# A density stage's tail: ScalarE writes the x term of two of three layer-1 sums into PSUM, with another order of the queues

## The chip, the cores and the metric

The kernel runs on one core of a Trainium2 chip. The metric is the device time of one execution in microseconds. Before the change it is 4800.04 us, the median of three runs (4797.65 to 4801.9). One further execution was profiled; every time by line or engine below is from it, counted from the start of its span.

## What is computed

The input x is 8 images of 192 channels and 64 x 64 pixels, in float32. Two layers follow each other, each with a residual:

```python
x = x + _L0_conv_ref(_gn(x), ...)   # softmax attention over the 4096 pixels
x = x + _L1_conv_ref(_gn(x), ...)   # density: a small network per channel
```

`_gn` is a group norm. The second layer is what the change touches. For every channel it evaluates a network of widths 1, 3, 3, 3, 1 at v - 0.5 and at v + 0.5 (v the normed value), and takes the difference of two sigmoids:

```python
for i in range(N_LAYERS):
    logits = jnp.einsum('cij,cjn->cin', jax.nn.softplus(ms[i]), logits) + bs[i]
    if i < N_LAYERS - 1:
        logits = logits + jnp.tanh(fs[i]) * jnp.tanh(logits)
...
likelihood = jnp.maximum(likelihood, 1e-06)
```

All weights are per channel, that is per partition: every product by a weight is a scale by a [128,1] operand, or, on TensorE, a matmul with a diagonal matrix.

## The kernel before, in words

A channel triple's three channels (g = 0, 1, 2) lie side by side on one of 64 partitions, and the two halves of the image fill 128 partitions. The attention of image b runs in 128 steps (16 steps for each of 8 blocks of 512 rows): scores (L780, PE), Exp (L784, ScalarE), row maxima for a later block (L708 on PE, L716 on VectorE) and the product with the values (L795, PE). The density of image b - 1 is worked off beside the attention of image b. The last image has nothing to run beside, so its density is the tail of the kernel.

The density of an image is 12 units, one for each chunk c of the image (2), g (3) and side s (lower or upper, 2); a unit's tiles are 128 x 1024. In the tail (`on_pe`, the last image) a unit does:

- u_j = tanh(w x + b), j = 0..2: three ScalarE operations (`tanh0`, L1015).
- Three layer-1 sums, one after the other (`product`, L988): sum i is the x term plus three u terms, each a matmul with a diagonal (`diag`, written by ScalarE at L877 and L885), for two halves of 512 columns: 4 x 2 = 8 matmuls, which the trace lists as 16 records. A sum fills two PSUM banks (a `[128, 2, 512]` tile). There are four such tiles in the tail (b0, b1, sc_tail, mx_tail), taken in turn.
- l1_i = tanh(sum i + bias) (`tanh1`, L996, ScalarE, PSUM to SBUF), then l1_i = tanh(f) * l1_i + sum i (`gate1`, L1006, VectorE), which gives the PSUM tile back.
- Three layer-2 sums: the first term with its offset is a ScalarE operation (`scaled`, L1040), the other two are VectorE's (`more`, L1047, in a dependent pair); then tanh (L1030) on ScalarE and the gate (`gate`, L1047 with `tf`).
- The layer-3 sum z: L1040 again and another pair at L1047.

When both sides of a (c, g) have their z, an ending follows. In the tail it is VectorE's and ScalarE's alone (`alone`): z0 + z1 (L1227, here the pair total), tanh of both (L1233), their difference and mask (L1239, L1240), Abs (L1249), and the store step (L1254), after which two DMAs on SP write the result. For the image before, whose last unit reaches into the tail, the last term of z comes from a ScalarE product (`plain`, L1072) that POOL adds in two halves (L1078), each preceded by a small memset (L1163) that waits for a recent VectorE operation.

Each engine runs its queue strictly in the order in which the program was written, so that order decides. It is made by a planner written in Python: `density_step` gives every engine a credit per emission step (`rate`, 4.15 in the tail) and each operation takes its cost (`COST`, in microseconds: DVE 1.22, ACT 1.23, TANH 1.05, PE 6.95). In the order ScalarE, PE, VectorE, up to four units are asked in turn to put operations out (`Unit.step`): the next one of a queue goes if what it needs was put out in an earlier step (VectorE's own results in the same step count as well), if a PSUM tile is free for a sum, and if, where it takes one of the 17 SBUF buffers, more are free than the older units still hold a claim to (`need`). `work_off` first runs what is due, such as endings, then `density_step` and `pool_step`, which puts out at most one waiting POOL piece per step.

```python
if makes and len(bufs) <= sum(u.need() for u in older) + len(endings):
    return
```

Of the kernel before, what the change touches and what calls it, by code (L numbers as in the profile page):

```python
# [10 lines left out]
AF = mybir.ActivationFunctionType  # L11
# [6 lines left out]
def kernel(  # L18
# [43 lines left out]
    nc = tc.nc  # L62

    B, C, H, W = x.shape
# [53 lines left out]
    for i in range(3):  # L118
        t = xin.tile([128, 3, P], F32, tag=f"xi{i}", name=f"xi{i}")
# [58 lines left out]
    for i in range(2):  # L178
        nc.vector.tensor_reduce(
            out=bb[i], in_=ident[:, 64 * i + CR : 64 * i + 64 : 32], axis=AX.X, op=ALU.add  # L180
# [6 lines left out]
    for s in range(2):  # L187
        p = slice(R * s, R * s + R)
# [4 lines left out]
    for i in range(2):  # L193
# [3 lines left out]
        for k in range(2):  # L197
            a = a2 if k == i else a1
            nc.scalar.dma_start(
                out=slope[i][64 * k : 64 * k + 64], in_=a.partition_broadcast(64)  # L200
# [33 lines left out]
    for src, dst, at, n in (  # L234
# [4 lines left out]
        for s in range(2):  # L239
            nc.sync.dma_start(  # L240
                out=dst[R * s : R * s + R, :, at : at + n],
# [91 lines left out]
    credit = {"DVE": 0.0, "ACT": 0.0, "PE": 0.0}  # L333
# [20 lines left out]
    for k in "ab":  # L354
        pair = []
        for i in range(2):
            u = work.tile([128, 2 * C], F32, tag=f"pr{k}{i}", name=f"pr{k}{i}")
# [60 lines left out]
    def work_off(t, rate):  # L418
        now[0] = t
        run_due(t)  # L420
        start_job(t)
        run_due(t)
        held = set()
        for kind, fn in list(loads):
            if free[kind] > 0 and kind not in held:
                loads.remove((kind, fn))
                fn()
            else:
                held.add(kind)
        density_step(t, rate)  # L430
        pool_step()
# [3 lines left out]
    norms = {}  # L435
# [169 lines left out]
    for i in range(2):  # L605
        t = dram.tile([NC, 64, F], F32, tag=f"qd{i}", name=f"qd{i}")
# [259 lines left out]
    COST = {"DVE": 1.22, "ACT": 1.23, "TANH": 1.05, "PE": 6.95}  # L866
    diag = []
    banks = deque()
    lower2 = mm.rearrange("p g n -> p (g n)")[:, 0:36].rearrange("p (s g i) -> p s g i", s=4, g=3)

    def diagonals(g, t):
# [36 lines left out]
    class Unit:  # L908
# [3 lines left out]
        def __init__(self, b, c, g, s):  # L912
            self.key = b, c, g, s
            self.at = {}
            self.buf = {}
            self.todo = {"DVE": deque(), "ACT": deque(), "PE": deque()}
            self.left = {"l": 6, "t": 9, "u": 0, "z": 1, "p": 1}
            self.held = {"l": 0, "t": 0, "u": 0, "z": 0, "p": 0}
            self.on_pe = b == B - 1
            add = self.add  # L920
            if self.on_pe:

                self.left.update(t=3, u=3, p=0)
                for i in range(3):
                    add("ACT", ("u", 0, i), [], self.tanh0, makes="u")
                for i in range(3):
                    add(
                        "PE", ("sum", i), [("u", 0, j) for j in range(3)], self.product,
                        frees=[("u", 0, j) for j in range(3)] if i == 2 else [],
                    )  # L930
                    add("ACT", ("l", 1, i), [("sum", i)], self.tanh1, makes="l")
                for i in range(3):
                    add("DVE", ("gate", 1, i), [("l", 1, i)], self.gate1)
            else:
                for i in range(3):
                    add("ACT", ("t", 0, i), [], self.tanh0, makes="t")
                    add("ACT", ("l", 1, i), [], self.linear, makes="l")
                for i in range(3):
                    for j in range(3):
                        add(  # L940
                            "DVE", ("mix", i, j), [("t", 0, j), ("l", 1, i)], self.mix,
                            frees=[("t", 0, j)] if i == 2 else [],
                        )
                    add("ACT", ("t", 1, i), [("mix", i, 2)], self.tanh, makes="t")
                for i in range(3):
                    add("DVE", ("gate", 1, i), [("t", 1, i)], self.gate, frees=[("t", 1, i)])
            for i in range(3):
                add("ACT", ("l", 2, i), [("gate", 1, 0)], self.scaled, makes="l")
                for j in (1, 2):
                    add("DVE", ("add", 2, i, j), [("gate", 1, j), ("l", 2, i)], self.more)  # L950
                add("ACT", ("t", 2, i), [("add", 2, i, 2)], self.tanh, makes="t")
            for i in range(3):
                add("DVE", ("gate", 2, i), [("t", 2, i)], self.gate, frees=[("t", 2, i)])
            add("ACT", ("l", 3, 0), [("gate", 2, 0)], self.scaled, makes="z")
            add("DVE", ("add", 3, 0, 1), [("gate", 2, 1), ("l", 3, 0)], self.more)
            if self.on_pe:
                add("DVE", ("add", 3, 0, 2), [("gate", 2, 2), ("l", 3, 0)], self.more)
            else:

                add("ACT", ("p", 3, 2), [("gate", 2, 2), ("add", 3, 0, 1)], self.plain, makes="p")  # L960

        def add(self, eng, name, after, fn, makes=None, frees=()):
            self.todo[eng].append((name, after, fn, makes, frees))
# [15 lines left out]
        def src(self):  # L979
            b, c, g, s = self.key  # L980
            return xc[b, c][:, g, :]

        def product(self, k):
            g, i = self.key[2], k[1]
            out = self.buf[k] = banks.popleft()
            for n, src in enumerate([self.src()] + [self.buf["u", 0, j] for j in range(3)]):
                for h in range(2):
                    nc.tensor.matmul(  # L988
                        out[:, h, :], lhsT=diag[g][:, 3 * i + n - 1 if n else 9 + i, :],
                        rhs=src[:, h * F : h * F + F], start=n == 0, stop=n == 3,  # L990
                    )

        def tanh1(self, k):
            b, c, g, s = self.key
# [99 lines left out]
        def need(self):  # L1094
            most = dict(self.left, t=max(0, min(self.left["t"], 1 - self.held["t"])))
            if ("add", 2, 2, 2) not in self.at:

                most.update(z=0, p=0)
            return sum(most.values())

        def step(self, eng, t, older):
            todo = self.todo[eng]
            while todo and credit[eng] > 0:
                name, after, fn, makes, frees = todo[0]
                if any(self.at.get(a, t) >= t for a in after if eng != "DVE" or a[0] in "ltu"):
                    return
                if eng == "PE" and not banks:
                    return
                if makes and len(bufs) <= sum(u.need() for u in older) + len(endings):
                    return  # L1110
                todo.popleft()
                if makes:
                    self.take(name, makes)
                fn(name)
                self.at[name] = t
                for k in frees:
                    self.give(k)
                credit[eng] -= COST["TANH" if name[0] == "t" and name[1] else eng]
# [35 lines left out]
    pieces = deque()  # L1154
# [3 lines left out]
    def pool_step():  # L1158


        if pieces:
            if len(recent) == 2:
                inst = nc.gpsimd.memset(pause, 0.0)  # L1163
                tc.add_manual_dep(
                    inst.ins, recent[0].ins.name,
                    mybir.DependencyInfo(
                        mybir.DependencyClass.Sync, mybir.DependencyReason.DATA
                    ),
                    reason="beside the reduce",
                )  # L1170
            pieces.popleft()()

    def ending(b, c, g):
# [46 lines left out]
        def alone():  # L1220

            s = cell["s"]
            parts = halves if (b, c, g) == (B - 1, 1, 2) else [slice(0, 2 * F)]

            def first():
                for n in parts:
                    nc.vector.tensor_tensor(s[:, n], z[0][:, n], z[1][:, n], ALU.add)  # L1227
                later(1, second, 0.0, 2.1)

            def second():  # L1230
                for n in parts:
                    for i in range(2):
                        nc.scalar.activation(z[i][:, n], z[i][:, n], AF.Tanh, scale=0.5)  # L1233
                later(1, third, 2.5)

            def third():
                for n in parts:
                    y = z[0][:, n]
                    nc.vector.tensor_tensor(y, z[1][:, n], y, ALU.subtract)  # L1239
                    nc.vector.scalar_tensor_tensor(y, s[:, n], 0.0, y, ALU.not_equal, ALU.mult)  # L1240
                bufs.extend((s, z[1]))
                later(1, lambda: size(parts), 0.0, 1.1)
                later(2, lambda: store(parts), 1.3)

            later(1, first, 1.25)
# [151 lines left out]
    RATE = 4.15  # L1397
    scores(0)()
    for t in range(last):
        b = t // IMG  # L1400
# [21 lines left out]
    t = last  # L1422
    homes[:] = [(turns[1], [0, 0])]
    while due or units or jobs or loads:

        work_off(t, RATE if (B - 1, 1) in norms else 1.3)
        t += 1
# [1 line left out]

# [36 lines left out]
```

## Time and profile before

| | us |
|---|---|
| median of three runs | 4800.04 |
| profiled execution | 4801.53 |
| its span | 4799.7 |
| PE busy in the span | 4653.4 (97%) |
| VectorE busy | 4179.0 (87%) |
| ScalarE busy | 3196.8 (67%) |
| POOL busy | 856.3 (18%) |
| first matmul of a layer-1 sum of the tail | at 4470.9 |
| last one | ends at about 4766.5 |
| first L1006 of the tail | at 4492.1 |
| first L1227 of the last image's endings | at 4572.6 |
| last L1227 | at 4788.9 |

Some 1.8 us of the profiled execution lie around its span. A line of the timeline has the start, the duration, the engine, the line of the kernel, the operation with its tiles, and in brackets how long the engine stood idle before it and who ended that. Lines are merged where one line's operations follow each other (x2, x3). Consecutive operations of an engine overlap by about 0.1 us, so the step from one start to the next is a little shorter than the duration. [...]

### The profile page before, as it was taken

What the parts mean: (1) busy time and instruction counts of PE and PEld (TensorE: products, weight loads), DVE (VectorE), ACT (ScalarE), POOL (GpSimd) and SP (SyncE); (2) the same over time, 40 slices, a digit from 0 to 9 for tenths busy, and PEclk for the clock granted to TensorE, in tenths of its full rate; (3) what the DMA queues carried; (4) which work ended last, traced back from release to release, by engine and by line L of the source; (5) the groups of instructions that cost most, each with busy time, mean ns of one, the idle gap of its engine ahead of it and who ended that gap; (6) DMA issues with size and microseconds to landing.
All of it is one profiled execution on the core that took longest, in us unless ns stands there. A gap on an engine that the chain in (4) does not pass through costs nothing.

```text
span 4799.7 us, 69014 instructions
## 1 busy us (share of the span) xinstructions
PE 4653.4 (97%) x28432; PEld 3440.0 (72%) x28432; DVE 4179.0 (87%) x4289; ACT 3196.8 (67%) x3665; POOL 856.3 (18%) x842
## 2 busy tenths in 40 slices
PE   7999999999999999999999999999999999999686
PEld 5777777777777777777777777777777777777332
DVE  5433359999999999999999999999999999998788
ACT  2333246777677767776777767777777777777675
POOL 0000001222122211221211221122222132222000
PEclk9999999999999999999999999999999999999898
DMA  2101020111110111010110111101111101000000
GB/s 58 41 18 29 18 48 14 35 28 29 42 27 25 37 39 34 27 44 9 36 46 26 33 40 33 32 19 33 36 38 33 34 13 27 10 12 16 9 13 13
DMA packets 109328, 138.60 MB, mean 29 GB/s; under 512 B 17106, under 2 KB 82132, under 8 KB 109012
## 3 DMA queue, kind: packets, MB, share of 16 engines
q1 hardware_dynamic: 107776, 133.81, 11.4%
q8 instruction: 223, 3.65, 0.3%
q14 instruction: 93, 0.76, 0.1%
q10 hardware_dynamic: 1236, 0.37, 0.0%
HBM read 100.58 MB, written 29.36 MB: 27 GB/s over the span
## 4 chain that ended last, share of the span: by engine, by line
PE 86%; DVE 7%; ACT 5%; issue 1%; DMA 0%; POOL 0%; ACTq 0%; SPq 0%; DVEq 0%; POOLq 0%
PE b L795 53%; PE sc L780 20%; PE b L669 4%; DVE d L1047 4%; PE b L988 2%; PE b L620 2%; DVE rm L716 1%; ACT d L1015 1%; ACT e L784 1%; PE mx_tail L988 1%; PE sc_tail L988 1%; PE b L828 1%; PE mx L708 1%; ACT d L1040 1%; PE b L745 0%
## 5 line engine op out<-in xcount | busy, mean ns | idle before, releaser
L795 PEld LDWEIGHTS b<-v,e 128*128 128x128 f32 x16384 | 2651.8, 190 | 776.9 <-issue 771.6
L795 PE MATMUL b<-v,e 128*128 128x193 f32 x16384 | 2955.7, 334 | 0.0
L784 ACT ACTIVATE e<-sc 128x1024 f32<-128x1024 f32 x1024 | 1045.9, 1021 | 1353.4 <-PE mx L708 1330.8
L716 DVE TENSOR_REDUCE rm<-mx 128x1 f32<-128x1024 f32 x1002 | 1222.3, 1220 | 481.4 <-PE mx L708 472.7
L780 PE MATMUL sc<-q,k 25*128 25x512 f32 x4096 | 1155.1, 640 | 24.2 <-ACT e L784 22.9
L708 PE MATMUL mx<-k,q 24*128 24x512 f32 x4008 | 1130.4, 640 | 0.6 <-DVE rm L716 0.6
L1047 DVE SCALAR_TENSOR_TENSOR d<-d,lc,d 128x1024 f32<-128x1024 f32 x756 | 986.1, 1314 | 12.2
L1047 DVE SCALAR_TENSOR_TENSOR d<-d,wsp,d 128x1024 f32<-128x1024 f32 x684 | 883.3, 1292 | 53.1 <-ACT d L1040 44.7
L1047 DVE SCALAR_TENSOR_TENSOR d<-d,tf,d 128x1024 f32<-128x1024 f32 x540 | 687.5, 1292 | 0.4 <-ACT d L1030 0.4
L1163 POOL MEMSET pause<- 128x1 f32 x408 | 40.0, 98 | 3613.2 <-DVE d L1047 3613.2
L1030 ACT ACTIVATE d<-d 128x1024 f32<-128x1024 f32 x540 | 568.2, 1054 | 42.6 <-DVE d L1047 40.8
L780 PEld LDWEIGHTS sc<-q,k 25*128 25x128 f32 x4096 | 306.2, 183 | 252.4 <-issue 175.8
L1040 ACT ACTIVATE d<-d,cb,wsp 128x1024 f32<-128x1024 f32 x348 | 429.9, 1236 | 4.3 <-DVE d L1047 3.3
L1015 ACT ACTIVATE d<-xc,bn,wn 128x1024 f32<-128x1024 f32 x288 | 354.0, 1236 | 7.7 <-issue 5.9
L1078 POOL TENSOR_TENSOR d<-d,d 128x512 f32<-128x512 f32 x168 | 331.8, 1975 | 47.7 <-ACT d L1072 46.6
L1024 ACT ACTIVATE d<-xc,bn,wn 128x1024 f32<-128x1024 f32 x252 | 311.8, 1237 | 0.0
L708 PEld LDWEIGHTS mx<-k,q 24*128 24x128 f32 x4008 | 299.8, 183 | 7.3 <-DVE rm L716 6.7
L1198 POOL TENSOR_TENSOR d<-d,d 128x512 f32<-128x512 f32 x80 | 173.0, 2163 | 0.0
L1210 POOL TENSOR_TENSOR d<-d,d 128x512 f32<-128x512 f32 x80 | 163.2, 2040 | 0.5 <-issue 0.5
L1218 POOL TENSOR_TENSOR d<-d,d 128x512 f32<-128x512 f32 x80 | 157.6, 1970 | 2.5 <-POOL pause L1163 0.9
L669 PE MATMUL b<-wv,xi 64*128 64x192 f32 x1344 | 139.5, 340 | 0.0
L669 PEld LDWEIGHTS b<-wv,xi 64*128 64x128 f32 x1344 | 106.5, 186 | 25.4 <-issue 21.5
(155 smaller groups left out, 2303.9 us busy)
## 6 DMA issues: line engine op xcount, KB each, us to landing
xi<-in_x_dram SPq DMA_DIRECT2D x280, 192.0 KB, 3.5
xc<-in_x_dram SPq DMA_DIRECT2D x64, 384.0 KB, 7.1
out_dram<-xc SPq DMA_DIRECT2D x94, 256.0 KB, 3.1
q<-qd SPq DMA_DIRECT2D x128, 128.0 KB, 2.7
k<-kq SPq DMA_DIRECT2D x64, 64.0 KB, 1.9
qd<-kq SPq DMA_DIRECT2D x64, 64.0 KB, 2.0
d<-in_x_dram SPq DMA_DIRECT2D x16, 192.0 KB, 4.1
out_dram<-xc SPq DMA_DIRECT2D x4, 128.0 KB
```

Source lines behind the costliest of these rows:

```text
L669: nc.tensor.matmul(pv[:, s, 0:C], lhsT=t[p, g, k * 128 : k * 128 + 128] if g < 3 else one_row[p], rhs=wf["v", b][p, g, :] if g < 3 else wf ...
L708: nc.tensor.matmul(sc[:, s, :], lhsT=tile_of(qt[b, n // 2], n, j)[r], rhs=kt[b][r, u : u + F], start=True, stop=True,)
L716: nc.vector.tensor_reduce(out=rowmax[b, n][:, j, k : k + 1], in_=sc, axis=AX.XY, op=ALU.max)
L780: nc.tensor.matmul(sc[:, s, :], lhsT=kt[b][r, k : k + 128], rhs=qt[b, n // 2][r, :, u : u + 256], start=True, stop=True,)
L784: return lambda: nc.scalar.activation(e, sc, AF.Exp)
L795: nc.tensor.matmul(a[:, j, 0 : C + 1], lhsT=e[:, s, j * 128 : j * 128 + 128], rhs=v[:, s, p % 4, :], start=p == 0 and s == 0 and j % 2 == ...
L1015: nc.scalar.activation(self.buf[k], self.src(), AF.Tanh, bias=bn[:, s, g, 0, i : i + 1], scale=wn[:, g, 0, i : i + 1],)
L1024: nc.scalar.activation(self.buf[k], self.src(), AF.Identity, bias=bn[:, s, g, 1, i : i + 1], scale=wn[:, g, 1, i : i + 1],)
L1030: nc.scalar.activation(self.buf[k], self.buf["l", k[1], k[2]], AF.Tanh)
L1040: nc.scalar.activation(self.buf[k], self.buf["l", n - 1, 0], AF.Identity, bias=offset, scale=wsp[:, g, w : w + 1],)
L1047: nc.vector.scalar_tensor_tensor(dst, src, factor, dst, ALU.mult, ALU.add)
L1078: return nc.gpsimd.tensor_tensor(z[:, n], z[:, n], dst[:, n], ALU.add)
```

## The change

In each unit of the tail, sums 1 and 2 get their x term from a new ScalarE operation, `fill`, which writes scale * x into the sum's PSUM tile; PE then adds the three u terms onto it without a start flag (6 matmuls instead of 8). The fill is put out only where the PSUM tile at the head of the row has already held a whole sum (`full`); otherwise `product` does all four terms. In the program that comes out, 22 of the 24 sums are filled. The fills of a unit stand after its sum 0, and each `tanh1` moves behind the fill of the next sum.

The other edits act on the order alone. `need` of a unit in the tail that has not put out its sum 2 claims `u` left plus 4 buffers, in place of all it will ever take. A fill takes its PSUM tile, so a sum that is filled needs no free one. A filled sum gives 1.7 of PE's credit back. An emission step in the tail gets 2.5 instead of 4.15. The first step of an ending in the tail puts out all waiting POOL pieces.

```diff
@@ Unit.__init__
                 for i in range(3):
+                    after = [("u", 0, j) for j in range(3)]
+                    if i:
+                        add("ACT", ("fill", i), [("sum", 0)], self.fill)
+                        after.append(("fill", i))
                     add(
-                        "PE", ("sum", i), [("u", 0, j) for j in range(3)], self.product,
+                        "PE", ("sum", i), after, self.product,
                         frees=[("u", 0, j) for j in range(3)] if i == 2 else [],
                     )
-                    add("ACT", ("l", 1, i), [("sum", i)], self.tanh1, makes="l")
+                    if i:
+                        add("ACT", ("l", 1, i - 1), [("sum", i - 1)], self.tanh1, makes="l")
+                add("ACT", ("l", 1, 2), [("sum", 2)], self.tanh1, makes="l")
@@ Unit
+        def fill(self, k):
+            b, c, g, s = self.key
+            i = k[1]
+            if id(banks[0]) in full:
+                out = self.buf["sum", i] = banks.popleft()
+                nc.scalar.activation(
+                    out, self.src().rearrange("p (h n) -> p h n", h=2), AF.Copy,
+                    scale=norms[b, 1][0][:, g, 1, i : i + 1],
+                )
+
         def product(self, k):
             g, i = self.key[2], k[1]
-            out = self.buf[k] = banks.popleft()
+            filled = k in self.buf
+            if not filled:
+                self.buf[k] = banks.popleft()
+            out = self.buf[k]
+            full.add(id(out))
             for n, src in enumerate([self.src()] + [self.buf["u", 0, j] for j in range(3)]):
+                if n == 0 and filled:
+                    continue
                 for h in range(2):
                     nc.tensor.matmul(
                         out[:, h, :], lhsT=diag[g][:, 3 * i + n - 1 if n else 9 + i, :],
                         rhs=src[:, h * F : h * F + F], start=n == 0, stop=n == 3,
+                        skip_group_check=filled,
                     )
+            if filled:
+                credit["PE"] += 1.7
@@ Unit.need
+            if self.on_pe and ("sum", 2) not in self.at:
+                return most["u"] + 4
             return sum(most.values())
@@ Unit.step
-                if eng == "PE" and not banks:
+                if not banks and (eng == "PE" and name not in self.buf or name[0] == "fill"):
                     return
@@ ending, alone, first
+                while pieces:
+                    pool_step()
@@ the loop of the tail
-        work_off(t, RATE if (B - 1, 1) in norms else 1.3)
+        work_off(t, 2.5 if (B - 1, 1) in norms else 1.3)
```

More of the change, by code (lines that the diff above doesn't have):

```diff
@@ L868 @@
     banks = deque()
+    full = set()
     lower2 = mm.rearrange("p g n -> p (g n)")[:, 0:36].rearrange("p (s g i) -> p s g i", s=4, g=3)
```

## The prediction

> **What bounds the kernel now.** I read the 40 slices first: only the last three (from 4440 us on) are the stage that the diff touches, and there neither engine is full.
>
> ```profile
> PE   7999999999999999999999999999999999999686
> DVE  5433359999999999999999999999999999998788
> ```
>
> The built programs agree: up to VectorE's first L1006 (4492.11 us in the trace) all engines have the same order, but for L885 blocks and one L996 that change places on ScalarE, and the waits of two POOL additions. So I split the tail (4462 to 4799.7) by engine.
>
> ```profile
> core 0: us, PE busy (x) PEld busy (x) DVE busy (x) ACT busy (x) POOL busy (x), PEclk, DMA share, GB/s
> 4462.00:4572.60 110.60, 79.05 (x166) 33.44 (x166) 89.92 (x93) 68.54 (x70) 9.05 (x8) 0.85 0.02 5
> 4572.60:4748.80 176.20, 160.98 (x372) 69.69 (x371) 154.43 (x128) 121.14 (x113) 0.00 (x0) 1.00 0.05 12
> 4748.80:4799.70 50.90, 17.70 (x42) 7.55 (x40) 38.43 (x36) 24.43 (x26) 0.00 (x0) 0.73 0.09 21
> ```
>
> In the even middle PE is busy 91%, VectorE 88%: close together, so PE's share proves nothing. VectorE's timeline there says what it waits for.
>
> ```profile
> 4634.52 2.60 DVE L1047 SCALAR_TENSOR_TENSOR d<-d,wsp,d 128x1024 f32<-128x1024 f32 x2
> 4639.38 2.60 DVE L1047 SCALAR_TENSOR_TENSOR d<-d,wsp,d 128x1024 f32<-128x1024 f32 x2 [2.25 <-ACT d L1040]
> 4641.90 1.27 DVE L1006 SCALAR_TENSOR_TENSOR d<-d,tf,sc_tail 128x1024 f32<-128x1024 f32 x1
> 4644.24 2.60 DVE L1047 SCALAR_TENSOR_TENSOR d<-d,wsp,d 128x1024 f32<-128x1024 f32 x2 [1.07 <-ACT d L1040]
> ...
> 4654.50 1.28 DVE L1006 SCALAR_TENSOR_TENSOR d<-d,tf,b 128x1024 f32<-128x1024 f32 x1 [0.36 <-ACT d L996]
> ...
> 4661.10 2.60 DVE L1047 SCALAR_TENSOR_TENSOR d<-d,wsp,d 128x1024 f32<-128x1024 f32 x2 [1.67 <-ACT d L1040]
> ```
>
> Three of four stalls come from L1040, which has nothing to do with PE: ScalarE's order puts tanh (L1030) of product pair i ahead of the L1040 that starts pair i+1, so VectorE waits a round trip. Only 0.36 (L996) comes from a PE sum. At the start of the stage it is different:
>
> ```profile
> 4497.50 1.88 PE L988 MATMUL mx_tail<-xc,v 128*128 128x512 f32 x4
> 4502.62 5.10 PE L988 MATMUL mx_tail<-d,v 128*128 128x512 f32 x8 [3.25 <-ACT d L1015]
> 4521.96 3.78 PE L988 MATMUL mx_tail<-d,v 128*128 128x512 f32 x4 [14.24 <-ACT d L1015]
> ```
>
> Unit 1's third u (L1015) is issued only at 4520.68: the code that writes the order kept buffers back for the older units. VectorE's first L1006 of unit 1 is therefore at 4527.66, and it idles between there and the first L1227 of the middle (4572.63).
>
> **The middle, part by part.** A period is two units, 45.28 us (L1227 at 4658.22 and 4748.79, two periods apart).
> PE: 22 sums lose the two x matmuls, four records of 0.43: 22 x 1.72 = 37.8 us in all; per period 6 x 6.87 = 41.2 becomes 34.3.
> ScalarE: 22 fills of 128x1024 from SBUF, scale by pointer, no bias, into PSUM. No row writes PSUM from ScalarE. Nearest is L1072, the same operation into SBUF:
>
> ```profile
> 4515.46 1.13 ACT L1072 ACTIVATE d<-d,wsp 128x1024 f32<-128x1024 f32 x1
> ```
>
> Bounds 1.04 (L1030, no pointer) and 1.24 (L1040, two). [...] I take 1.13, following step 1.04.
> VectorE: the same operations in another order. Steps from one start to the next: product or add pair 2.51, L1006 1.19, gate 1.2, the four ending operations 1.14, 1.26, 1.14, 1.14. Per period 6 x 1.19 + 6 x 2.51 + 6 x 1.2 + 2 x 2.51 + 4.68 = 39.1; today's stalls are 45.28 - 39.1 = 6.2 (the five idles of a period, 5.7, plus 0.08 of lost overlap at each).
>
> Now the new order, walked from the start of unit A's first L1006 (= 0), B being the next unit; ScalarE steps 1.13 (L1015, L1040), 1.02 (L996), 0.95 (tanh, Abs), hand-over 0.04. The third L1006 is at 2.99 (below), so pair 1 ends at 6.8.
> - Pair 2 waits for tanh 1 and L1040: 0.04 + 0.95 + 1.23 + 0.04 after the end, less 0.08 overlap: stall 2.34. As before.
> - Pair 3: one L1006 (1.19) lies in the round trip: 1.15. As before. The fill between L1040 and L996 starts when pair 2 does and has 0.7 us of slack before the next tanh.
> - B's pair 2: the pair total L1227's 1.14 now covers part, and only one u stands ahead of tanh instead of three: 1.2 (before 1.67 + 0.08).
> - B's pair 3: difference and mask lie in it (2.4); the fill behind the ending's two tanh makes ScalarE 0.17 late: 0.1 (the mask waited 0.37 before).
> - A's third sum is where the new wait binds. The fill stands behind B's last L1040, so it runs 39.7 to 40.8; twelve matmul records 40.9 to 46.3; L996 to 47.4; the L1006 could start at 46.9 and starts at 47.5: stall 0.6 (0.36 + 0.08 before). Behind that fill on ScalarE are L996 and three L1015, all with slack.
> Sum 2.34 + 1.15 + 1.2 + 0.1 + 0.6 = 5.4; period 39.1 + 5.4 = 44.5. The middle gains 0.8 per period, not the 6.9 that PE is relieved of.
>
> [...] The rows: after idle of 3.25 (above) eight records took 5.10 instead of 3.70; in the middle, after 1.75 to 2.75, none slowed. The walk gives PE gaps of 5.2 us ahead of A's second sum and at most 2.8 ahead of the third. The second has its L996 in line only at 40.6 while its sum is done at 37.9, so up to 2.5 us are hidden; and its slowness shortens the gap ahead of the third. [...] I take zero: 2.75 did nothing.
>
> **The start.** In the new order unit 1's u stand at 4501.4, 4510.7 and 4511.8 on ScalarE, ahead of older units' operations, each of which they make up to 1.13 later (in the walk). Walking both queues on from 4493.4 with the same steps (and one extra microsecond for a VectorE operation beside a POOL addition, as at 4520.55, which took 2.30): pair additions on POOL now wait for VectorE operations of 4514.3 and 4522.6, so the leftover L1227 is at 4524.9 (4526.5 before). Unit 1's L1006: 4526.1, 4533.4, 4536.7 (before 4527.7, 4534.6, 4540.9); the fills at 4518.6 and 4528.1, each with its 5.15 of matmuls, have one to two microseconds of slack before their L996. Unit 2's: 4546.0, 4553.0, 4557.9 (before 4549.5, 4554.6, 4561.6). Here the gain opens up: unit 1's last add pair is at 4555.3 instead of 4566.45, and L1227 at 4561.6 instead of 4572.6: 11.0 us, of which 2.5 only because two products that stood ahead of it now come after (they are paid in the next interval).
>
> **Free edits.** The skipped group check, the credit and the shorter step (2.5 for 4.15) emit nothing; they act through the order, costed above. SP's order of DMAs is the same, and L1254, which releases each store, keeps its place relative to the endings. Diagonals of group 1 (L885, 0.97) move ahead of an L1040: 0.25 later, hidden by the L1047 that run until 4488.7. The last unit: after the third L1006 its chain has no neighbours before or after; 4788.9 to 4799.7 stays, the interval before it goes from 40.1 to 39.5.
>
> **Sum against the profiled execution (span 4799.7, 4801.53 in all).** First L1227 4561.6; four periods of 44.5 = 177.9 (44.48 unrounded); last interval 39.5; end 10.8: 4789.8, that is 9.9 us less. The median shown (4800.04) is 1.5 below the profiled execution; the same 9.9 off it gives 4790.1, -0.21%.
>
> **Rivals.**
> - PE was the bound after all: all 37.8 us come back where PE is back to back, some 4762 to 4775. For it: PE at 91%, and ScalarE's L996 waiting 58 us for PE between 4540 and 4740; against it: VectorE's own waits are L1040 round trips, in an order that stays. 7%.
> - [...] 12%.
> - The start doesn't gain: POOL's second addition or the trickle of u keeps L1227 4 to 6 us later: 4794 to 4796. For it: this is the longest walk, over states that the trace never showed. 12%.
> - Slower: the fill is slow. With e us over 1.13 it adds e at A's third sum, e at B's third pair and e - 0.7 at A's third pair, 2.3 per period at e = 1, and about 10 over the stage, so gain and loss balance near 2.1 us; at 2.9 us it adds about 20 and the kernel takes 4810, slower by over 0.2%. For it: no row of such a write. Against: no 128x1024 row of ScalarE is over 1.24. 7%.
> - The walk holds within 3 us: 62%.
>
> **Numbers.** 0.2%, about what a measurement of this kernel can tell from no change, is 9.6 us, or 4790.4, and my forecast lies on that line. Of the walk's 62% some 38 fall below it and 24 above; with 7% from the PE case: faster 0.45; same 0.48 with the cold and start cases; slower 0.07. The range takes in walk, start and most of the cold case: 4785 to 4798.
>
> **What would show it.** Period between L1227s 44.5; VectorE stalls from L1040 still 2.25 and 1.07; a fill mean of 1.05 to 1.15; PE busy about 77% of the middle with a gap near 5 us per period; first L1227 of the middle at 4561 to 4562. I am wrong if the period is under 43 (PE did bind), or over 45.3, or the first L1227 is past 4565.

## The result, and the profile after

The changed kernel takes 4790.71 us (median of 20 runs, 4788.74 to 4794.94) against 4799.59 for the kernel before beside it: a ratio of 0.9981, 95% interval 0.9975 to 0.9988. Its profiled execution took 4788.83, with a span of 4787.0.

Two executions start the tail at slightly different times: the first matmul of a layer-1 sum is at 4470.91 before and at 4467.20 after, although what stands ahead of it is the same. I therefore measure the tail from that matmul to the end of the span: 328.79 before, 319.80 after, **8.99 less**. The lines of the code have moved: gate1 (L1006 before) is now L1035, the product pairs (L1047) L1076, their first term (L1040) L1069, tanh1 (L996) L1025, the sums' matmuls (L988) L1014, u (L1015) L1044, the pair total (L1227) L1262. The fill is L998.

The 40 slices: PE is as full as before, VectorE one step fuller at the end.

```profile
PE   7999999999999999999999999999999999999686
DVE  5433359999999999999999999999999999999888
```

The tail in three stretches, cut at the first pair total and at the last but one (columns as before):

```profile
core 0: us, PE busy (x) PEld busy (x) DVE busy (x) ACT busy (x) POOL busy (x), PEclk, DMA share, GB/s
4462.00:4558.04 96.04, 70.29 (x140) 28.80 (x141) 83.68 (x88) 68.15 (x70) 8.94 (x8) 0.87 0.02 6
4558.04:4736.38 178.34, 153.91 (x326) 64.89 (x324) 156.98 (x129) 142.66 (x132) 0.00 (x0) 0.92 0.05 12
4736.38:4787.00 50.62, 13.53 (x25) 5.37 (x24) 38.54 (x36) 26.01 (x27) 0.00 (x0) 0.67 0.09 21
```

The middle holds four periods of 44.58 (45.28 before). PE's 326 records there (372 before, in a window 2 us shorter) still keep it busy 86%, because its granted clock has fallen to 0.92 and some of them follow each other at half the pace (rows below). From the first layer-1 matmul to the first pair total of the middle it is 90.84 (101.72 before): **10.88 less, all in the start**. The next interval gives 4.29 of it back (44.59, before 40.30, since products that stood ahead of that total now come behind it), the three periods that follow bring 2.1, and the last interval 0.30 (39.81, before 40.11). The end is 10.81 (10.80).

VectorE's timeline of one period, from one pair total to the next:

```profile
4602.63 1.22 DVE L1262 TENSOR_TENSOR d<-d,d 128x1024 f32<-128x1024 f32 x1
4604.97 2.60 DVE L1076 SCALAR_TENSOR_TENSOR d<-d,wsp,d 128x1024 f32<-128x1024 f32 x2 [1.12 <-ACT d L1069]
...
4622.77 1.28 DVE L1035 SCALAR_TENSOR_TENSOR d<-d,tf,b 128x1024 f32<-128x1024 f32 x1 [0.57 <-ACT d L1025]
...
4628.82 2.60 DVE L1076 SCALAR_TENSOR_TENSOR d<-d,wsp,d 128x1024 f32<-128x1024 f32 x2 [2.25 <-ACT d L1069]
...
4633.68 2.61 DVE L1076 SCALAR_TENSOR_TENSOR d<-d,wsp,d 128x1024 f32<-128x1024 f32 x2 [1.06 <-ACT d L1069]
```

The round trips through ScalarE (L1069) are all still there. The 0.57 ahead of the third gate is the new wait: that sum's fill, then its matmuls, then its tanh.

PE, in the start and in the middle:

```profile
4508.05 5.37 PE L1014 MATMUL mx_tail<-d,v 128*128 128x512 f32 x8 [7.28 <-ACT d L1044]
...
4585.26 5.42 PE L1014 MATMUL b<-d,v 128*128 128x512 f32 x12 [1.46 <-ACT b L998]
...
4607.88 13.64 PE L1014 MATMUL b<-d,v 128*128 128x512 f32 x24 [5.19 <-ACT b L998]
```

Unit 1's last u now ends a wait of PE at 4508.05, where before it did so at 4521.96. In the middle PE waits for the fills: 5.19 ahead of the second sum, and the 24 records behind that gap take 13.64. The two sums from 4585.26 on, at full clock, take 10.57, so the slow matmuls behind the gap cost 3.07.

The fills themselves, by destination; this is the row of one PSUM tile (count, then shortest, median and longest in ns):

```profile
L998 ACT ACTIVATE b<-xc,wn x11: 1097/1098/1099, 4513.6 to 4722.7; 128x1024 f32<-128x1024 f32 x11
```

### The profile page after: what moved, and what is told of

It reads as the page before. It is cut to its first block, busy times and chain, and to the rows that moved or that the text cites. A ratio compares the mean times of both kernels' runs of the same rounds, so it can differ in the third digit from the quotient of the medians.

```text
span 4787.0 us, 68872 instructions
## 1 busy us (share of the span) xinstructions
PE 4629.4 (97%) x28344; PEld 3425.8 (72%) x28344; DVE 4178.5 (87%) x4289; ACT 3220.9 (67%) x3687; POOL 856.9 (18%) x842
## 4 chain that ended last, share of the span: by engine, by line
PE 83%; DVE 8%; ACT 6%; issue 2%; DMA 0%; POOL 0%; POOLq 0%; SPq 0%; ACTq 0%; DVEq 0%
PE b L795 53%; PE sc L780 20%; DVE d L1076 6%; PE b L669 4%; PE b L620 2%; DVE rm L716 1%; ACT e L784 1%; ACT d L1044 1%; PE b L828 1%; ACT d L1069 1%; PE mx L708 1%; PE b L1014 1%; ACT d L1059 1%; PE mx_tail L1014 0%; PE b L745 0%
## 5 line engine op out<-in xcount | busy, mean ns | idle before, releaser
L1076 DVE SCALAR_TENSOR_TENSOR d<-d,lc,d 128x1024 f32<-128x1024 f32 x756 | 987.6, 1316 | 12.2
L1076 DVE SCALAR_TENSOR_TENSOR d<-d,wsp,d 128x1024 f32<-128x1024 f32 x684 | 883.5, 1292 | 54.1 <-ACT d L1069 45.7
L1076 DVE SCALAR_TENSOR_TENSOR d<-d,tf,d 128x1024 f32<-128x1024 f32 x540 | 685.7, 1289 | 0.4 <-ACT d L1059 0.4
L1069 ACT ACTIVATE d<-d,cb,wsp 128x1024 f32<-128x1024 f32 x348 | 430.0, 1236 | 5.1 <-DVE d L1076 3.5
L1044 ACT ACTIVATE d<-xc,bn,wn 128x1024 f32<-128x1024 f32 x288 | 354.6, 1237 | 7.7 <-issue 5.9
L1014 PE MATMUL b<-d,v 128*128 128x512 f32 x216 | 105.7, 643 | 21.4 <-ACT b L998 18.7
```

The costliest lines, as they stand in the source:

```text
L1044: nc.scalar.activation(self.buf[k], self.src(), AF.Tanh, bias=bn[:, s, g, 0, i : i + 1], scale=wn[:, g, 0, i : i + 1],)
L1069: nc.scalar.activation(self.buf[k], self.buf["l", n - 1, 0], AF.Identity, bias=offset, scale=wsp[:, g, w : w + 1],)
L1076: nc.vector.scalar_tensor_tensor(dst, src, factor, dst, ALU.mult, ALU.add)
```

## The experiments

My theory: VectorE's waits set the tail's length, most of them round trips in ScalarE's order; PE's relief is worth nothing. The main rival: PE was the bound and the fill is what gained. "Tail" below is the time from the first layer-1 matmul to the end of the span in the profiled execution (before 328.79, changed kernel 319.80); "period" is from one pair total to the next.

**The changed kernel's order without its fills**

```diff
-                nc.scalar.activation(out, ..., scale=norms[b, 1][0][:, g, 1, i : i + 1])
...
-                if n == 0 and filled:
-                    continue
```

> The changed kernel's order on every engine, but the 22 fills are left out of ScalarE's queue and PE does all four terms of every sum (the same result by the old way). My theory (VectorE's round trips behind L1069 set the period, PE does not): the stalls 2.25, 1.06 and 1.12 stay, the one ahead of the third sum's gate (0.57) shrinks to 0.2 or less because that sum no longer waits for a fill, so a two-unit period of 43.8 to 44.2 instead of 44.58, though PE has its 41.2 of matmuls per period back: about 4788, that is 2 to 4 less than the changed kernel. Rival (the relief of PE is what gained): the period goes back to 45.3 or more and the time to 4796 to 4800. Rival (the fill is neutral): within 1 of 4790.7.

Measured: 4785.67 (ratio to the kernel before 0.9970, 0.9959 to 0.9982), tail 314.54, periods 43.84 to 43.89. PE has its 22 x 1.72 = 37.8 us back and the kernel is 5 us *faster* than the changed one. VectorE's own waits from 4490 to 4780 (whom it waited for, us in total, times, longest) say where. In the changed kernel:

```profile
DVE d L1076 <- ACT d L1069: 29.8, 19, 2.3
DVE d L1035 <- ACT d L1025: 5.6, 9, 1.8
```

and without the fills, where the same two lines of code are L1069 and L1028:

```profile
DVE d L1069 <- ACT d L1062: 30.3, 19, 2.3
DVE d L1028 <- ACT d L1018: 0.9, 1, 0.9
```

The round trips stay, the waits for a sum's tanh go from 5.6 to 0.9. VectorE and ScalarE run the same operations in the same order in both traces, the fills apart. The rival has fallen, and the fill costs 5.26 of tail: 1.67 in the start, 2.84 in four periods, 0.77 in the last interval.

**The shorter step alone, on the kernel before**

```diff
-        work_off(t, RATE if (B - 1, 1) in norms else 1.3)
+        work_off(t, 2.5 if (B - 1, 1) in norms else 1.3)
```

> The kernel before with one edit, the emission step of the tail 2.5 instead of 4.15. The start of its order is that of the changed kernel up to unit 1's sums, and the middle has one kind of period in which the pair total comes later. My prediction put the start's 11.0 on the count of held buffers. If that is right, this kernel keeps the first pair total at about 101.7 after the tail's first matmul and takes 4796 or more. If the shorter step brings it, the first pair total is near 91 and the time 4788 to 4794.

Measured: 4779.79 (0.9957, 0.9945 to 0.9970), tail 308.90, first pair total of the middle at 88.00, then intervals of 40.30, 42.70, 42.65, 42.81. That is under both ranges that I had given. One number in the planner gives 20 us, and all that the change adds to it loses 11 of them. Unit 1's u stand where they stand in the changed kernel (the first 30.3 after the first layer-1 matmul in both), so the shorter step is enough to make the start. In the middle, the gate that the changed kernel has ahead of the pair before the total lies behind the total:

```profile
4597.30 1.22 DVE L1227 TENSOR_TENSOR d<-d,d 128x1024 f32<-128x1024 f32 x1
4598.44 1.27 DVE L1006 SCALAR_TENSOR_TENSOR d<-d,tf,sc_tail 128x1024 f32<-128x1024 f32 x1
4599.63 2.60 DVE L1047 SCALAR_TENSOR_TENSOR d<-d,wsp,d 128x1024 f32<-128x1024 f32 x2
```

So a gate (L1006, at 4598.44) lies in the round trip that the changed kernel sits out for 1.12 (at 4604.97 above). With the two others left, 39.1 + 2.34 + 1.15 = 42.6.

**The fill alone, with the old step and the old count**

```diff
-        work_off(t, 2.5 if (B - 1, 1) in norms else 1.3)
+        work_off(t, RATE if (B - 1, 1) in norms else 1.3)
...
-            if self.on_pe and ("sum", 2) not in self.at:
-                return most["u"] + 4
```

(the pieces put out at an ending go too.)

> The fill and its place between sums and tanh, but the step of 4.15, the old count of held buffers and the pieces as before. My theory (PE's relief gains nothing, order does): first pair total at 100 to 104 after the tail's first matmul, as before, a period of 44.5 to 46, in all 4797 to 4804, no faster than before by more than 3. Rival (PE's relief gains): at least 6 of the 8.9 are here, 4794 or less.

Measured: 4799.34 (0.9998, 0.9990 to 1.0007), tail 326.62, intervals of 48.50, 39.58, 45.73, 45.53. No gain that can be told from none, as expected. Its first pair total came at 96.06, earlier than the 100 to 104 that I expected, but its intervals are uneven, and in all its tail is 2.2 shorter.

**Each fill twice**

```diff
+                for _ in range(2):
                     nc.scalar.activation(
```

> The changed kernel with each fill issued twice, into the same tile: 22 more ScalarE operations of 1.1 (steps of 1.04). My theory: the fill is on the path at A's third sum, at B's third pair and, past 0.7 of slack, at A's third pair: 1.0 + 1.0 + 0.3 = 2.3 per period and 9 to 11 over the stage, about 4801. Rival (ScalarE, at 67%, has room): under 3 in all, 4791 to 4794.

The second write repeats the first. Measured: 4810.46 (1.0020, 1.0012 to 1.0028), tail 339.01, periods of 47.89. That is 19.2 for 22 operations with a step of 1.04: 84% of the added ScalarE time shows at the end, about twice what I expected. The period of this kernel on VectorE:

```profile
4634.92 1.28 DVE L1036 SCALAR_TENSOR_TENSOR d<-d,tf,b 128x1024 f32<-128x1024 f32 x1 [1.72 <-ACT d L1026]
...
4644.16 1.28 DVE L1036 SCALAR_TENSOR_TENSOR d<-d,tf,sc_tail 128x1024 f32<-128x1024 f32 x1 [0.58 <-ACT d L1026]
...
4651.44 1.28 DVE L1036 SCALAR_TENSOR_TENSOR d<-d,tf,mx_tail 128x1024 f32<-128x1024 f32 x1 [0.21 <-ACT d L1026]
...
4656.65 1.28 DVE L1036 SCALAR_TENSOR_TENSOR d<-d,tf,b 128x1024 f32<-128x1024 f32 x1 [0.22 <-ACT d L1026]
...
4668.86 2.61 DVE L1077 SCALAR_TENSOR_TENSOR d<-d,wsp,d 128x1024 f32<-128x1024 f32 x2 [1.16 <-ACT d L1070]
```

The waits I had priced are there: 1.72 instead of 0.57, the pair at 1.16, and 0.58 (of which the next pair gives 0.26 back), 2.6 in all for my 2.3. I had missed the two gates at 0.21 and 0.22 and the overlap lost at three new stalls (0.24), which makes 3.3. The start adds 3.7 and the last interval 2.3.

**The three edits of the order, no fill** (step 2.5, the count, the pieces; on the kernel before)

> The kernel before with the three edits that only move the order (step 2.5, the count of held buffers, the pieces put out at an ending) and no fill. The shorter step alone took 4779.8. If the count of held buffers and the pieces bring little, this lies within 4 of it, 4776 to 4784, with periods of 42.3 to 43.2. If they are what costs the changed kernel its 11 against the step alone, it lies at 4786 or more.

Measured: 4780.74 (0.9959, 0.9946 to 0.9973), tail 310.11, periods of 42.88 to 43.06. As expected, without the fill the count and the pieces add nothing to the shorter step (308.90).

**The shorter step and the fill, without the count and the pieces**

```diff
-            if self.on_pe and ("sum", 2) not in self.at:
-                return most["u"] + 4
...
-                while pieces:
-                    pool_step()
```

> The changed kernel without the count of held buffers and without the pieces put out at an ending: the shorter step and the fill alone. VectorE's order is that of the changed kernel, ScalarE's has the fills at other places. If the fill is what makes the changed kernel slower than the step alone (by standing in ScalarE's queue, and by the order that it makes the planner choose), this takes 4788 to 4794, periods 44.2 to 45. If the count of held buffers does, it takes 4780 to 4784.

Measured: 4806.85 (1.0017, 1.0010 to 1.0023), tail 334.05, periods of 47.4 to 47.7: slower than the kernel before, and worse than either theory had it. VectorE's order is that of the changed kernel; ScalarE's differs. PE and VectorE in the period that corresponds to the one above:

```profile
4614.27 12.14 PE L1014 MATMUL b<-d,v 128*128 128x512 f32 x24 [9.35 <-ACT b L998]
```

```profile
4627.66 1.28 DVE L1035 SCALAR_TENSOR_TENSOR d<-d,tf,b 128x1024 f32<-128x1024 f32 x1 [3.40 <-ACT d L1025]
```

Here the second sum's fill stands behind the ending's tanh and Abs on ScalarE and starts 8.3 after the pair total; in the changed kernel it stands ahead of Abs and starts 4.1 after it. PE waits 9.35 instead of 5.19, and the third gate 3.40 instead of 0.57: 2.8 to 3.2 more in each of four periods, 2.9 in the last interval. So beside the shorter step the count (or the pieces) is worth 14 of tail with the fill and nothing without it. The two were not tried apart; the pieces act on POOL, which does nothing in the middle, so the count is the likelier of the two, but that is not shown.

**The shorter step, no fill, and each product's first term ahead of the tanh before it**

```diff
             for i in range(3):
-                add("ACT", ("l", 2, i), [("gate", 1, 0)], self.scaled, makes="l")
+                if not (self.on_pe and i == 2):
+                    add("ACT", ("l", 2, i), [("gate", 1, 0)], self.scaled, makes="l")
+                if self.on_pe and i == 1:
+                    add("ACT", ("t", 2, 0), [("add", 2, 0, 2)], self.tanh, makes="t")
+                    add("ACT", ("l", 2, 2), [("gate", 1, 0)], self.scaled, makes="l")
...
-                add("ACT", ("t", 2, i), [("add", 2, i, 2)], self.tanh, makes="t")
+                if not (self.on_pe and i == 0):
+                    add("ACT", ("t", 2, i), [("add", 2, i, 2)], self.tanh, makes="t")
```

> The step of 2.5 and no fill, and on ScalarE each product's first term (L1040) put ahead of the tanh of the product before it, so that VectorE has the next pair to do while that tanh runs. The stalls of 2.25 and 1.06 should go. VectorE's own work is 39.1 per period, PE's 41.2 with all four terms: PE should now bind, periods of 41.2 to 42.0 with PE gaps near nothing, and some 4772 to 4777. If VectorE's stalls behind L1040 were not what the period is made of, it stays at 42.7 and 4780.

Measured: **4765.39** (0.9926, 0.9914 to 0.9938), tail 294.42, intervals of 41.36, 40.21, 40.96, 42.27. This beats both kernels, by 34 and 25 us, and is lower than the 4772 that I expected at best: of the 14.5 by which its tail is shorter than with the step alone, 8.2 are in the start (first pair total at 79.81). VectorE's waits for a product's first term from 4490 to 4780, with the step alone and here (the same two lines of code):

```profile
DVE d L1047 <- ACT d L1040: 25.7, 15, 2.3
DVE d L1052 <- ACT d L1045: 1.1, 1, 1.1
```

The four periods between its pair totals:

```profile
core 0: us, PE busy (x) PEld busy (x) DVE busy (x) ACT busy (x) POOL busy (x), PEclk, DMA share, GB/s
4549.40:4714.20 164.80, 164.80 (x386) 72.96 (x385) 155.92 (x130) 126.30 (x116) 0.00 (x0) 1.00 0.05 13
```

PE is busy in every microsecond, at full clock, and four times 41.2 is 164.8. With the round trips gone, PE *is* the bound of these periods.

**The same, plus the fill as in the change** (without the count and the pieces)

> As the one with the product's first term ahead, plus the fill. If PE's 41.2 per period is the bound there, the fill (34.3) lets the period fall towards VectorE's 39.1: 39.2 to 40.5, some 3 to 10 less than the kernel without the fill, 4764 to 4772. If the fill's place in ScalarE's queue costs as it did in the changed kernel, the period is 41.5 or more and the fill brings nothing or a loss here too.

Measured: 4792.69 (0.9986, 0.9979 to 0.9993), tail 325.40, periods of 46.9 to 49.5. Where PE binds and loses 17% of its matmuls, the kernel becomes 27 us slower, and VectorE waits for the sums' tanh: 39.5 us in 16 waits from 4490 to 4780, against 4.0 in 4 without the fill. Two of them (gate1 is L1040, tanh1 L1030 here):

```profile
4621.64 1.28 DVE L1040 SCALAR_TENSOR_TENSOR d<-d,tf,b 128x1024 f32<-128x1024 f32 x1 [3.52 <-ACT d L1030]
4626.78 1.28 DVE L1040 SCALAR_TENSOR_TENSOR d<-d,tf,b 128x1024 f32<-128x1024 f32 x1 [3.87 <-ACT d L1030]
```

**The count of held buffers alone, on the kernel before**

> The kernel before with one edit, the count of held buffers. The shorter step alone brought the start's gain and more; my prediction had put the late u of unit 1 on buffers kept back. If the count alone changes next to nothing without the fill: first pair total 100 to 103 after the tail's first matmul, periods 44.5 to 45.5, 4796 to 4801. If it is a second way to the same gain: first pair total at 88 to 92 and under 4790.

Measured: 4794.11 (0.9989, 0.9982 to 0.9995), tail 323.67, first pair total at 100.51, periods of 44.30. The start is as expected the old one; the periods are 0.2 shorter than I allowed for and the time is 1.9 under the range. So on the kernel before the count alone is worth 5.1 of tail, 1.2 of it in the start. The rows with unit 1's third u, with the shorter step and with the count:

```profile
4508.57 2.36 ACT L1015 ACTIVATE d<-xc,bn,wn 128x1024 f32<-128x1024 f32 x2
```

```profile
4521.09 2.36 ACT L1015 ACTIVATE d<-xc,bn,wn 128x1024 f32<-128x1024 f32 x2
```

They begin 39.6 and 49.8 after the first layer-1 matmul; the changed kernel has 39.6 there, the kernel before 49.8.

**One fill per unit, or two, put out with the sum's own matmuls**, on the kernel with the first term ahead, whose order stays as it was on every engine:

```diff
             out = self.buf[k] = banks.popleft()
+            filled = i == 1 and id(out) in full
+            full.add(id(out))
+            if filled:
+                b, c, _, s = self.key
+                nc.scalar.activation(out, ..., scale=norms[b, 1][0][:, g, 1, i : i + 1])
```

(`i > 0` for two; a filled sum leaves out its x matmuls.)

> The kernel with the step of 2.5 and the product's first term put ahead (4765.4, periods of 41.2 on average, PE without a gap), its order kept on every engine, plus one fill per unit, for sum 1 alone, written at the sum's own place in the order and not at the end of the sum before it. PE has 37.8 per period then, VectorE 39.1. If relieving PE is worth something only where PE binds, and the fill costs nothing where PE stands in a queue of its own: periods of 39.2 to 40.6 and 4756 to 4763. If a fill in ScalarE's queue always holds up a tanh that VectorE waits for: 41.2 or more and 4765 or more.

> The same with both fills per unit, for sums 1 and 2. PE 34.3 per period, ScalarE about 34. VectorE's 39.1 bounds it from below, so at best equal to the kernel with one fill; PE has gaps here and may run at half clock after them, and the second fill waits for a tile that a gate has to free first. I expect 40 to 42.5 per period and 4760 to 4772; if the number of fills doesn't matter, it equals the kernel with one within 1.

Measured: 4866.26 (1.0136, 1.0122 to 1.0150) with one and 4917.57 (1.0243, 1.0229 to 1.0257) with two. Both expectations are missed widely. ScalarE with one fill (L996; tanh1 is L1013), and the PE line that it releases:

```profile
4612.69 1.10 ACT L996 ACTIVATE b<-xc,wn 128x1024 f32<-128x1024 f32 x1
4622.00 1.11 ACT L1013 ACTIVATE d<-b,bn 128x1024 f32<-128x1024 f32 x1 [8.21 <-PE b L1004]
```

```profile
4613.84 8.06 PE L1004 MATMUL b<-d,v 128*128 128x512 f32 x12 [7.81 <-ACT b L996]
```

The fill stands directly ahead of its own sum's tanh in ScalarE's queue. PE, which would have run this sum during the 7.81 before, starts it when ScalarE gets there; then ScalarE sits 8.21 with nothing but that tanh at the head of its queue. PE's lead over ScalarE is gone, once per unit. Slow matmuls are part of it (8.06 in place of 5.42 here): over the eleven gaps of the kernel with one fill they add some 23 us, at most a quarter of the 99 by which its tail is longer than without fills.

**One fill per unit, earlier in the queue**: the same, but put out right behind sum 0's matmuls

```diff
+            if i in (0,) and banks and id(banks[0]) in full:
+                b, c, _, s = self.key
+                seed = self.buf["sum", i + 1] = banks.popleft()
+                nc.scalar.activation(seed, ..., scale=norms[b, 1][0][:, g, 1, i + 1 : i + 2])
```

> Again the kernel with the step of 2.5 and the product's first term put ahead (4765.4), plus one fill per unit, for sum 1, but put out right after sum 0's matmuls: in ScalarE's queue it stands ahead of sum 0's tanh, some 6 us of ScalarE work ahead of its own tanh, where the late one stood directly in front of it (4866). A filled sum cannot start before ScalarE has come to its fill. If that distance is what decides, twelve matmuls of 5.3 now fit in it: periods of 39.3 to 41.2, 4756 to 4766. If a fill ties PE to ScalarE's queue at any place here, PE loses its lead all the same and it takes 4770 or more.

Measured: 4782.66 (0.9963, 0.9950 to 0.9977), tail 309.64, intervals of 42.15, 42.45, 47.32, 46.22. The expectation is missed, and its second theory holds. The distance takes back 84 of the 101 us, and still the kernel is 17 us slower than without a fill, with the same order of VectorE's and ScalarE's other operations. The fill (L1008) and its matmuls:

```profile
4622.38 1.10 ACT L1008 ACTIVATE mx_tail<-xc,wn 128x1024 f32<-128x1024 f32 x1
```

```profile
4623.54 7.11 PE L1000 MATMUL mx_tail<-d,v 128*128 128x512 f32 x12 [2.84 <-ACT mx_tail L1008]
```

ScalarE reaches the fill late because the tanh ahead of it waits for a pair on VectorE; PE waits 2.84, and its twelve records then take 7.11 in place of 5.42. Behind five of the eleven fills the matmuls are slow in this way, 1.7 each: at most 8.5 of the 15 by which the tail is longer. So the fill's cost hangs on its place, and the place depends on everything ahead of it in ScalarE's queue; how the cost divides between waiting and slow matmuls is not shown.

## Why the prediction was right, point by point

The time (4790.1 predicted, 4790.71 measured) came out by the steps that were to give it, but one cause was wrong. That the two are only 0.6 apart is in part luck: the gain was 1.0 smaller than forecast (8.88 between the medians), and the median from which I started was 0.45 above the 4799.59 measured beside the changed kernel.

**What bounds the kernel: right.** Giving PE its matmuls back makes the changed kernel faster (tail 314.54 against 319.80), and taking VectorE's round trips away makes PE the bound (164.80 of 164.80).

**The middle: right.** Period 44.58 for 44.5. The stalls are 2.25, 1.06, 1.12 and, at A's third sum, 0.57; with the 0.08 of lost overlap at each that is 2.33, 1.14, 1.20 and 0.65, for 2.34, 1.15, 1.2 and 0.6. The runs split the 0.7 that a period gains: the order gives 1.4 (45.28 to 43.88) and the fill takes 0.7 back.

**The fill: 1.098 for 1.13.** L1101, the same operation into SBUF, is 1.13 in the tail of this trace too, so the fill into PSUM is 0.03 shorter.

**The clock: right in the sum, poor in its reason.** The gap of 5.2 ahead of the second sum came (5.19). The slow matmuls behind it (records 0.85 us apart, not 0.43) cost 3.07. Nearly all of it is hidden by ScalarE's queue: the slow sum ends about 0.1 after the third sum's fill, which is the 44.58 in place of 44.48. The cold case, the third sum slow like this in each period at 8 us in all, is one of the two rivals at 12% and the 4798 at the top of my range. No run shows those 8: the third sum had no gap in the four periods (0.18 in the last interval), so the case was never put to the test. What the runs show in its place is the 3.07 at the second sum, all but 0.1 of it hidden. But "2.75 did nothing" was a poor reason: in these runs gaps of 2.12 (the kernel without fills), 2.23 (the changed kernel) and 2.84 (one early fill) were followed by twelve records of 7.11, while 2.75 (before, and with the fill alone) and once 3.27 (one early fill) were not:

```profile
4662.96 7.11 PE L1008 MATMUL b<-d,v 128*128 128x512 f32 x12 [2.12 <-ACT d L1037]
```

```profile
4536.41 5.42 PE L1000 MATMUL mx_tail<-d,v 128*128 128x512 f32 x12 [3.27 <-ACT mx_tail L1008]
```

The length of the gap alone does not decide it here between 2.1 and 3.3. PE's share of the middle, 86% in place of my 77%, is mostly the same thing: four slow stretches of 3.1 count as busy.

**The start: right in size (10.88 for 11.0), wrong in cause.** I said that "the code that wrote the order kept buffers back for the older units". The shorter step alone moves unit 1's u to where they are in the changed kernel and the first pair total to 88.0; the count alone leaves the u where they were and the first pair total at 100.5. What in the planner holds these u back at the longer step is not shown. The walk of the changed order itself held: counted from the first layer-1 matmul, unit 1's u and six gates came within 1.4 of it and the pair total within 0.2. Two misses of opposite sign help it to that: the leftover pair total came 1.3 before its place in the walk, and unit 1's third sum took 7.11, not 5.15. I had listed the step as an edit that acts "through the order, costed above" and never asked which edit made the order.

**The sum:** 9.9 predicted from the first layer-1 matmul on, 8.99 measured: the start gained 0.1 less, each of four periods 0.1 less and the last interval 0.3 less; the rest is rounding.

**The rivals.** PE as the bound, a cold third sum, a start that gains nothing: none came. The slow fill did not come either, but I had sized its slope at half: another 1.04 per fill costs 3.3 per period and 19.2 in all, not 2.3 and 10. What failed there is the list of places, "e at A's third sum, e at B's third pair and e - 0.7 at A's third pair": two more gates had less than 1 us of slack.

**What the prediction did not see** is where the gain of this change comes from. By tails:

| edits | tail, us |
|---|---|
| none (before) | 328.79 |
| fill | 326.62 |
| count | 323.67 |
| step | 308.90 |
| step, count, pieces | 310.11 |
| step, fill | 334.05 |
| step, count, pieces, fill (the change) | 319.80 |

The shorter step is worth 19.9. With it, the fill costs 25 alone and 9.7 with the count and the pieces (27 and 10 by the medians of the runs). Of those 9.7, the changed kernel's order without its fills (314.54) puts 5.3 on the fills themselves and 4.4 on the order that the planner chooses because of them.

## What to carry to other kernels

Work moved off a busy engine onto another engine's queue can cost more by its place there than by its duration: here one fill of 1.1 us per unit cost 101 us in one place and 17 in another, and one of those in the first place made PE wait 11.34 us (for the sum at 4585.35), because PE could no longer run ahead of ScalarE. The duration counts too: of a second write per fill, 84% came out at the end. Ask first which engine's waits set the period, in that engine's own list of waits; here the share of busy time said who binds only when they were gone, by setting one operation ahead of another. And when a change bundles edits of an order with a new operation, run each alone: the one-number edit was worth more than twice the whole.

## What I had not expected of the hardware

PE's matmuls fall to half pace (records 0.85 us apart, not 0.43) after quite different gaps. Where the matmuls ahead had run at full pace, idle of up to 1.90 us (the fill alone) in the tails of these runs never slowed those behind it, and from 3.38 (each fill twice) to 14.24 (before) it always did; between 2.1 and 3.3 us the same length did and did not (2.12, 2.23, 2.60 and 2.84 did, 2.35, 2.52, 2.68, 2.75 and 3.27 did not, and 2.88 did in the kernel without fills but not in the changed one). Nor does the gap set the price: in the changed kernel 2.99 and 5.19 cost 3.05 and 3.07, and 4.04 cost 1.7, its slow matmuls coming only after two records at nearly full pace. What else decides it beside the gap's length is not shown. A fill of 128 x 1024 into PSUM took 1.097 to 1.100 us in each of 22 cases.
